# A decoder layer on one core: other DMA layouts for its weights and for queries and keys, and a redrawn order of work

## The chip, the cores and the metric

The kernel runs on one core of one Trainium2 chip. The metric is the device time in microseconds, lower is better. A core has TensorE (PE, with its weight loads as PEld), VectorE (DVE), ScalarE (ACT), GpSimd (POOL) and SyncE (SP), which here issues every DMA. SBUF is the on-chip memory, PSUM the accumulator memory of PE.

## The reference, cut to what matters

The input `x` is 16 sequences of 256 rows of 512 float32 numbers. The layer adds three things to it, one after the other:

```python
x = x + attn(layernorm(x), q_w, q_b, k_w, k_b, v_w, v_b, o_w, o_b)       # 16 heads of 32, causal
x = x + xattn(ctx_2048, ctx_2048, layernorm(x), ssm_kernel, D, 8)
x = x + ffn(layernorm(x), w_gate_up, w_down)

# attn: q = x @ q_w.T + q_b, likewise k, v; softmax(q k^T / sqrt(32) + causal mask) @ v, then @ o_w.T + o_b
# xattn: per head h (8 rows i, j): kv[i,j] = k[i] * v[j]; y = causal convolution of kv with ssm_kernel[h]
#        out[j] = sum_i (y[i,j] + D[h] * kv[i,j]) * q[i]
# ffn: activations and weights rounded to 8 bits per row; silu(gate) * up, then down
```

## The kernel before, in words

The work has two halves. In the first, 16 batches of attention are cut into 64 units `(b, g)`: a batch of 256 rows and a group of four heads. In the second, 32 tiles of 128 rows go through the convolution and the FFN. Beside the attention the pair products `kv` of the convolution are made (`pairs_*`) and the FFN weights are rounded and turned (`weight_*`).

At the start the four projection weights are loaded in float32 (`proj_in`, `wl_q` to `wl_o`, 1 MB each), squared and summed on ACT for a bound of their size (`proj_norm`), from which scales come (`scale_top`, `scale_all`: short DVE instructions and two tiny matmuls). Each weight is turned on PE against an identity (`proj_turn`, sixteen 128x128 blocks), and written to SBUF as the sum of two float16 parts: `proj_hi` on ACT and `proj_lo` on DVE. Every projection is then three matmuls, high times high, high times low, low times high (`mm3`).

For each batch the rows are loaded (`norm_load`, step `xi`), normalised (`norm_stats`, `norm_rows`), split into a high part on ACT (`turn_hi`, `xh`) and a low part on POOL (`turn_lo`, `xl`), and both are turned by a DMA (`turn_out`, steps `("xo", b, 0)` and `("xo", b, 1)`, into `xhT` and `xlT`). Finished rows are stored by `out_store` (`os`); the buffer `xt` of a batch is one of three.

For each unit, `project_mm` computes queries and keys, `project_hi` and `project_lo` split them in two float16 parts each (`qkhl`, four planes of 128x256), `project_store` writes them to DRAM (`qk_d`, step `qs`), and `project_stack` reads them back in five DMAs into `st` (`qt`), where the parts of 32 rows stand above each other so that one matmul of 96 rows gives the scores. Then come softmax, the turning of the probabilities and the weighted sum.

The order of the instructions on every engine is not written by hand. Each step is given to a planner (`Plan.add`) with its engine, a due time (`when`), a planned duration, the steps it comes after, and the buffers it takes. `Plan.order` walks planned time; whenever an engine is free it starts the ready step with the earliest due time. The program is emitted in that order, so each engine's queue, that of SP among them, is fixed by it. With `T = 8.8` planned microseconds a unit, batch `b` has `t = 4 * T * b`; steps of the changeover and the second half follow from `B2 = 64 * T`. A table `shift` then moves the due times: for every kind of step (the first part of its key and the length of the key) one value for each range of `when`, the ranges cut at `bounds`:

```python
for s in pl.steps:
    if isinstance(s["key"], tuple):
        v = shift.get((s["key"][0], len(s["key"])))
        s["when"] += v[sum(s["when"] >= b for b in bounds)] if v else 0.0
```

An argument `after=` makes a step wait for another's end with its DMA landed; `then=` only for the other's issue.

Of the kernel before, what the change touches and what calls it, by code (L numbers as in the profile page):

```python
# [11 lines left out]
F16 = mybir.dt.float16  # L12
I32 = mybir.dt.int32
AF = mybir.ActivationFunctionType
# [94 lines left out]
def kernel(  # L109
# [433 lines left out]
    if True:  # L543
# [50 lines left out]
        def proj_in(nm):  # L594
            wl = wld.tile([P, KC, D], F32, name=f"wl_{nm}")
            nc.sync.dma_start(wl, dict(q=q_w, k=k_w, v=v_w, o=o_w)[nm].rearrange("(o p) i -> p o i", p=P))
            wraw[nm] = wl
# [17 lines left out]
        def scale_top(j):  # L615
# [6 lines left out]
            nc.vector.tensor_scalar(t2[:, 2:4], idf[:2, :2], t2[:, 1:2], None, ALU.mult)  # L622
# [5 lines left out]
        def scale_all(j):  # L628
# [8 lines left out]
            nc.vector.tensor_tensor(bias[:, j:j + 2, :], bias[:, j:j + 2, :], ap(sc, j, [[1, 2], [0, KC]]), ALU.mult)  # L637
# [9 lines left out]

        def proj_hi(nm, kc):
            nc.scalar.activation(wT[nm][0][:, kc, :], wps[nm, kc], AF.Copy, scale=sc[:, 2, names.index(nm):names.index(nm) + 1])

        def proj_lo(nm, kc):
            hi, lo = wT[nm]
            nc.vector.scalar_tensor_tensor(
                lo[:, kc, :], wps.pop((nm, kc)), sc[:, 2, names.index(nm):names.index(nm) + 1], hi[:, kc, :],
                ALU.mult, ALU.subtract)
# [119 lines left out]
        def project_store(b, g):  # L775
            pjs.pop(("qk", b, g))
            qk_d = dram.tile([4, P, S], F16, tag="qk_d", bufs=4, name=f"qk_d{b}_{g}")
            nc.sync.dma_start(qk_d.rearrange("n p s -> p n s"), qks.pop((b, g)))
            qkd[b, g] = qk_d

        def project_stack(b, g, n):
            if n == 0:
                stks[b, g] = ap2.tile([96, 2, 4, S], F16, tag="st", bufs=STB, name=f"st{b}_{g}")
            r3, first, n, src = ((0, 0, 2, 1), (1, 0, 1, 1), (1, 1, 1, 3), (2, 0, 1, 0), (2, 1, 1, 2))[n]
            nc.sync.dma_start(
                stks[b, g][32 * r3:32 * r3 + 32].rearrange("r j h s -> r (j h) s")[:, 4 * first:4 * first + 4 * n, :],
                bass.AP(qkd[b, g].tensor, qkd[b, g].offset + src * P * S, [[S, 32], [32 * S, 4 * n], [1, S]]))


        def scores_mm(b, g, qc, h2):  # L790
# [8 lines left out]
            for hh in range(2):  # L799
                nc.tensor.matmul(  # L800
                    ps[:, hh, :nk], stk[:, 0, 2 * h2 + hh, qc * P:(qc + 1) * P], stk[:, 1, 2 * h2 + hh, :nk],
# [279 lines left out]
        for n, nm in enumerate(names):  # L1081
            j = n // 2
            pl.add(("pi", nm), "SP", -80 + 10 * n, 0.55, proj_in, nm, late=1.5, dma=3.3)
# [73 lines left out]
        def batch(b):  # L1157
            t = KC * T * b
            xt = ("xt", b)
            if True:  # L1160
                pl.add(("xi", b), "SP", t - 9.5 * T, 0.44, norm_load, b, late=1.9, dma=1.5, new=[xt])
                if b == 0:
                    pl.add("ob", "SP", -45, 0.5, bias_rows, late=2.0, dma=0.8)
# [117 lines left out]
        for i in range(NT):  # L1281
# [76 lines left out]
        bounds = (60,330,570,680,1010)  # L1358
        shift = {
            ("bi", 2): (0.8, 5.7, 3, 5.9, 1.9, 8.6),  # L1360
            ("bk", 3): (14.4, 12.2, -4.6, 11.1, 15.6, 13.5),
            ("bn", 2): (-4.8, 0.7, 13.6, -2.3, -10.8, 2.5),
            ("bp", 2): (0.2, -9, 3.2, 0, 2.1, 3.1),
            ("bq", 2): (8.5, -3.6, 0.7, 0.7, -24, 0.7),
            ("br", 2): (6.5, 6.7, 1.5, 1.5, -20.1, 1.5),
            ("bs", 2): (0.5, 0.5, 12, 0.5, 20.5, 11.6),
            ("bt", 2): (-3.1, 4.5, 6, 10.4, -3.2, -23.3),
            ("ck", 2): (-1.3, -3.1, -0.1, 0.4, -3.2, -0.3),
            ("cl", 3): (-2.5, 1.1, -0.3, 2.3, -4.4, 1.3),
            ("cm", 2): (-3.9, -1.5, -4.7, -1, -1.5, -4.8),  # L1370
            ("cm", 3): (-3.3, -0.5, 5.2, 4.4, 7.2, -7.4),
            ("co", 2): (-2.8, 5.1, -9.1, 6.1, -12.9, -12.1),
            ("cr", 2): (-4.6, 3.8, -1.4, 0.3, 0.6, 8),
            ("cs", 3): (-7.5, -6, -24.7, -8.3, -15.4, -9.2),
            ("ct", 3): (2, 2.5, 0.3, 0.3, 5.3, -0.5),
            ("cu", 3): (0.2, 1.3, -10.5, -7.1, -6.1, 10.5),
            ("cw", 2): (-1.4, 14, 15.9, -13.5, -1.4, -10.2),
            ("cx", 2): (-27.7, -25.8, -20.3, 0.1, -26.2, -22.6),
            ("cz", 2): (-0.6, 1.6, 0.1, -1.1, 0.1, 0.1),
            ("dm", 2): (9.4, 21.8, 4.5, 11.7, 42.3, 23.4),  # L1380
            ("do", 2): (6.5, -0.8, -1, -6.8, -0.7, -20.7),
            ("dr", 2): (17.3, 17, 7.9, 9, 24.4, 14.2),
            ("ds", 2): (-1.2, -1.7, 7, -1.7, -3.6, 4.7),
            ("fc", 3): (-1.3, 2.5, -6.8, -2.3, 1.7, 1.8),
            ("fd", 2): (-0.3, 0.4, -7.3, 2.9, 0.4, -2.9),
            ("fm", 2): (-14, -14, -17.7, -12.3, -15.4, -10.3),
            ("fm", 3): (1.6, 0.8, -2.2, -0.7, 6.5, 3.9),
            ("fn", 2): (0.2, 0.9, -0.7, 0.2, 2, -4.5),
            ("fo", 2): (2.3, -7.2, 16.2, 3.2, 1.4, -7.2),
            ("fp", 2): (6.6, -2.6, 6.6, -1.9, -11, -3.8),  # L1390
            ("fq", 2): (0.8, -4.2, 0.7, -3, 5.5, 0.8),
            ("fr", 2): (-4.7, 2.6, -0.2, 8.5, 5.7, -28.6),
            ("fs", 2): (-0.1, -20.6, -16.5, 0.2, -23.3, -16.9),
# [106 lines left out]
```

## Time and profile before

| | |
|---|---|
| time, median of 3 runs | 1157.89 us (1155.21 to 1161.72) |
| profiled execution | 1164.23 us, of which the span is 1162.4 us |
| PE busy | 1076.4 us (93%) |
| DVE busy | 1015.8 us (87%) |
| POOL busy | 947.5 us (82%) |
| ACT busy | 838.0 us (72%) |
| DMA | 229.48 MB in 269026 packets |

The profile is one execution. Its span is the time between the first and the last instruction, and the execution's own time lies 1.8 us above it. Busy is the share of the span in which an engine has at least one instruction under way. Matmuls overlap: one of 256 columns is recorded at about 0.27 us, while the next starts 0.11 us later, so a busy PE is not yet PE at its peak. The first matmul of the convolution starts at 621.6 us.

### The profile page before, as it was taken

The numbers are of one execution on the slowest core, as the hardware profiler recorded it, in microseconds if no ns is written. First come the engines' busy times: TensorE is split into PE (matmuls) and PEld (weight loads), VectorE is DVE, ScalarE is ACT, GpSimd is POOL, SyncE is SP. The second block draws the span as 40 slices with busy tenths as digits, with TensorE's granted clock in tenths as the row PEclk, the third lists the DMA queues.
The fourth block names the chain that finished last, engine by engine and source line by source line (L and its number), as shares of the span: only waits on it lengthen the run. The fifth ranks groups of instructions, "written<-read, shape, count | busy, mean of one in ns | idle before, by whom it ended". The sixth has DMA issues, their size and how long they took to land.

```text
span 1162.4 us, 25593 instructions
## 1 busy us (share of the span) xinstructions
PE 1076.4 (93%) x8503; PEld 766.8 (66%) x8503; DVE 1015.8 (87%) x3188; ACT 838.0 (72%) x1999; POOL 947.5 (82%) x924
## 2 busy tenths in 40 slices
PE   4999889999999989999999889999999999999965
PEld 3766657776667756776666666767767667766632
DVE  5999678888788877987787999999999999999997
ACT  6898878898998878998885456575556566655444
POOL 4497888889999966899514799999999999999962
PEclk9999999999999999999999999999999999999989
DMA  7687798888888977879548956657666766676422
GB/s 244 166 226 246 207 225 219 246 262 229 229 245 233 264 215 199 251 228 258 172 145 274 280 153 189 186 148 192 168 175 169 186 167 168 174 187 156 102 48 66
DMA packets 269026, 229.48 MB, mean 197 GB/s; under 512 B 125177, under 2 KB 223519, under 8 KB 268767
## 3 DMA queue, kind: packets, MB, share of 16 engines
q1 hardware_dynamic: 268895, 227.85, 70.4%
q8 instruction: 67, 1.10, 0.4%
q14 instruction: 64, 0.52, 0.1%
HBM read 124.10 MB, written 75.74 MB: 172 GB/s over the span
## 4 chain that ended last, share of the span: by engine, by line
DVE 32%; PE 31%; POOL 13%; ACT 9%; DMA 8%; issue 5%; SPq 2%; DVEq 0%; POOLq 0%; ACTq 0%
DVE hp L450 4%; PE g L425 4%; ACT p L816 3%; DVE s L454 3%; DVE u L338 3%; DVE p L809 3%; PE pj_qk L659 3%; PE pj_qk L658 3%; PE pj_qk L660 3%; DMA xlT<-xl 2%; DVE u L341 2%; PE c L324 2%; PE c L326 2%; PE c L325 2%; POOL g L443 2%
## 5 line engine op out<-in xcount | busy, mean ns | idle before, releaser
L816 ACT ACTIVATE p<-p,nmax 128x256 f32<-128x256 f32 (+1 forms) x512 | 230.0, 454 | 11.3 <-DVE nmax L809 10.7
L809 DVE CUSTOM_DVE_ANT_0 p<-s,mask,esc 128x128 f32<-128x128 f32 (+1 forms) x512 | 187.1, 411 | 14.8 <-PE s L800 14.6
L324 PE MATMUL c<-bkv,T 128*128 128x288 f16 x640 | 183.2, 286 | 9.4 <-issue 3.2
L325 PE MATMUL c<-bkv,T 128*128 128x288 f16 x640 | 183.1, 286 | 0.0
L326 PE MATMUL c<-bkv,T 128*128 128x288 f16 x640 | 183.0, 286 | 0.0
L425 PE MATMUL g<-w,xq 128*128 128x384 bf16 (+1 forms) x1024 | 169.1, 315 | 13.1 <-DVE o L528 6.3
L964 POOL TENSOR_TENSOR kv<-p,kv 128x1152 f16<-128x1152 f32 x64 | 152.0, 2382 | 7.9 <-ACT kv L959 7.8
L946 POOL TENSOR_TENSOR p<-kT 128x1024 f32<-128x1024 f32 x64 | 143.9, 2249 | 2.3
L425 PEld LDWEIGHTS <-xq 128*128 128x128 bf16 x1024 | 100.4, 98 | 68.0 <-issue 8.1
L443 POOL TENSOR_TENSOR g<-g,sw 128x704 f32<-128x704 f32 x60 | 101.0, 1705 | 3.9 <-ACT g L436 3.9
L816 ACT ACTIVATION_READ_ACCUMULATOR p<-p,nmax 128x1 f32 x512 | 100.4, 196 | 0.0
L800 PE MATMUL s<-st 96*128 96x128 f16 (+1 forms) x512 | 84.5, 247 | 8.9 <-DVE nmax L809 8.4
L338 DVE TENSOR_TENSOR u<-c,qT 128x512 f32<-128x512 f32 x128 | 87.3, 682 | 5.9 <-PE c L326 5.3
L766 ACT ACTIVATE qkhl<-pj_qk,bias 128x256 f16<-128x256 f32 x128 | 59.8, 469 | 45.3 <-PE pj_qk L660 33.7
L771 DVE SCALAR_TENSOR_TENSOR qkhl<-pj_qk,bias,qkhl 128x256 f16<-128x256 f32 x128 | 59.9, 478 | 33.5 <-ACT qkhl L766 21.0
L827 POOL TENSOR_SCALAR lb<-lsum 128x256 f32<-128x256 f32 x64 | 26.0, 406 | 75.6 <-DVE lsum L823 48.9
L357 POOL TENSOR_TENSOR u<-u 128x512 f32<-128x512 f32 x60 | 76.9, 1282 | 9.6 <-DVE u L338 9.6
L510 PE MATMUL d<-w,hq 128*128 128x512 bf16 x352 | 80.9, 379 | 3.8 <-DVE hp L450 3.0
L324 PEld LDWEIGHTS <-T 128*128 128x128 f16 x640 | 62.6, 98 | 29.1 <-DVE u L344 5.9
L659 PE MATMUL pj_qk<-xlT,wq_hi 128*128 128x256 f16 x256 | 70.5, 275 | 10.7 <-DMA xlT<-xl 10.7
L841 PE MATMUL pt<-idf,p 128*128 128x128 f32 x524 | 79.9, 275 | 0.0
L658 PE MATMUL pj_qk<-xhT,wk_hi 128*128 128x256 f16 x256 | 70.0, 273 | 7.3 <-ACT qkhl L766 6.9
(236 smaller groups left out, 3326.1 us busy)
## 6 DMA issues: line engine op xcount, KB each, us to landing
kv_d<-kv SPq DMA_DIRECT2D x64, 576.0 KB, 3.5
bkv<-kv_d SPq DMA_DIRECT2D x64, 576.0 KB, 3.9
qk_d<-qkhl SPq DMA_DIRECT2D x64, 256.0 KB, 2.9
st<-qk_d SPq DMA_DIRECT2D x256, 64.0 KB, 2.7
T<-pad_d SPq DMA_DIRECT2D x64, 256.0 KB, 4.2
x_d<-xt SPq DMA_DIRECT2D x32, 256.5 KB, 3.5
bx<-x_d SPq DMA_DIRECT2D x32, 256.5 KB, 3.6
xt<-in_x_dram SPq DMA_DIRECT2D x16, 512.0 KB, 4.2
```

Of the source, the lines that this page charges most:

```text
L324: nc.tensor.matmul(reg, T[:, 0, d:d + P], kv[:, mi, 0, :], start=mi == 0, stop=False)
L325: nc.tensor.matmul(reg, T[:, 0, d:d + P], kv[:, mi, 1, :], start=False, stop=False)
L326: nc.tensor.matmul(reg, T[:, 1, d:d + P], kv[:, mi, 0, :], start=False, stop=mi == li)
L338: nc.vector.tensor_tensor(ap(u, uo, [[UW, 2], [64, 4], [1, 64]]), ap(pc, 0, [[512, 2], [64, 4], [1, 64]]), ap(qT, qo, [[96, 2], [8, 4], [1 ...
L425: nc.tensor.matmul(pg[:, :c.stop - c.start].rearrange("p (r o) -> p r o", o=P), t["xq"][:, kc, :], w1[:, (o + c.start) // P:(o + c.stop) / ...
L443: (nc.gpsimd if i < NT - 2 else nc.vector).tensor_tensor(ts[i]["g1"][:, c], ts[i]["g1"][:, c], sw1[:, I + c.start:I + c.stop], ALU.mult)
L658: nc.tensor.matmul(ps, lh, rh, start=first, stop=False)
L659: nc.tensor.matmul(ps, lh, rl, start=False, stop=False)
L809: nc.vector.tensor_tensor_reduce(out=prs[b, g][qc][:, h, :], in0=ps[:, hh, :nk], in1=mask2[:, P - qc * P:2 * P], op0=ALU.add, op1=ALU.min, ...
L816: nc.scalar.activation(pr[:, h, :], pr[:, h, :], AF.Exp, scale=-1.0, bias=nmax[:, qc, h:h + 1], accum_out=lsum[:, qc, h:h + 1])
L946: nc.gpsimd.tensor_tensor(ap(p, 0, [[NKV, 4], [64, 4], [1, 64]]), ap(kT, o, [[96, 4], [0, 4], [1, 64]]), ap(kT, o, [[96, 4], [8, 4], [1, 6 ...
L964: nc.gpsimd.tensor_tensor(kv[:, :, 1, :], p, kv[:, :, 0, :], ALU.subtract)
```

## The change

Seven edits:

1. `proj_in` puts row `4p + o` of a weight into partition `p`, where before it was row `128o + p`. A partition's four rows are then one piece of 8 KB in DRAM, where they were four of 2 KB. The turned blocks hold every fourth column, and `proj_hi` and `proj_lo` write (and read `hi`) with a step of four float16 elements, so that `wT` is as before.
2. The load of the output weights is issued after the first batch's `xlT` transpose: `then=[("xo", 0, 1)]` for the fourth weight.
3. `qk_d` is laid out `[128, 4, 256]` in place of `[4, 128, 256]`: a partition's four planes are one piece of 2 KB.
4. `st` is laid out `[96, 4, 2, 256]`, heads before query and key, so that the stack read which takes two planes has pieces of 1 KB; the four others keep pieces of 512 B, now 2 KB apart in DRAM.
5. Two multiplications by a scale use `scalar_tensor_tensor` with a broadcast operand in place of `tensor_scalar` and `tensor_tensor`.
6. The planner is told 2.9 instead of 3.3 us of DMA for a projection weight, and 2.0 instead of 0.5 us of SP for `ob`.
7. `bounds` has two cuts more, at -50 and 10, and all values of `shift` are others.

```diff
-            nc.sync.dma_start(wl, dict(q=q_w, k=k_w, v=v_w, o=o_w)[nm].rearrange("(o p) i -> p o i", p=P))
+            nc.sync.dma_start(wl, dict(q=q_w, k=k_w, v=v_w, o=o_w)[nm].rearrange("(p o) i -> p o i", p=P))
...
-            nc.vector.tensor_scalar(t2[:, 2:4], idf[:2, :2], t2[:, 1:2], None, ALU.mult)
+            nc.vector.scalar_tensor_tensor(t2[:, 2:4], idf[:2, :2], 1.0, ap(t2, 1, [[0, 2]]), ALU.mult, ALU.mult)
...
-            nc.vector.tensor_tensor(bias[:, j:j + 2, :], bias[:, j:j + 2, :], ap(sc, j, [[1, 2], [0, KC]]), ALU.mult)
+            nc.vector.scalar_tensor_tensor(bias[:, j:j + 2, :], bias[:, j:j + 2, :], 1.0, ap(sc, j, [[1, 2], [0, KC]]), ALU.mult, ALU.mult)
...
+        def cols(t):
+            return t.rearrange("k (p o) -> k o p", o=KC)
+
         def proj_hi(nm, kc):
-            nc.scalar.activation(wT[nm][0][:, kc, :], wps[nm, kc], AF.Copy, scale=sc[:, 2, names.index(nm):names.index(nm) + 1])
+            nc.scalar.activation(cols(wT[nm][0][:, kc, :]), wps[nm, kc].rearrange("k (o p) -> k o p", o=KC), AF.Copy,
+                                 scale=sc[:, 2, names.index(nm):names.index(nm) + 1])
...
-                lo[:, kc, :], wps.pop((nm, kc)), sc[:, 2, names.index(nm):names.index(nm) + 1], hi[:, kc, :],
-                ALU.mult, ALU.subtract)
+                cols(lo[:, kc, :]), wps.pop((nm, kc)).rearrange("k (o p) -> k o p", o=KC),
+                sc[:, 2, names.index(nm):names.index(nm) + 1], cols(hi[:, kc, :]), ALU.mult, ALU.subtract)
...
-            qk_d = dram.tile([4, P, S], F16, tag="qk_d", bufs=4, name=f"qk_d{b}_{g}")
-            nc.sync.dma_start(qk_d.rearrange("n p s -> p n s"), qks.pop((b, g)))
+            qk_d = dram.tile([P, 4, S], F16, tag="qk_d", bufs=4, name=f"qk_d{b}_{g}")
+            nc.sync.dma_start(qk_d, qks.pop((b, g)))
...
-                stks[b, g] = ap2.tile([96, 2, 4, S], F16, tag="st", bufs=STB, name=f"st{b}_{g}")
-            r3, first, n, src = ((0, 0, 2, 1), (1, 0, 1, 1), (1, 1, 1, 3), (2, 0, 1, 0), (2, 1, 1, 2))[n]
+                stks[b, g] = ap2.tile([96, 4, 2, S], F16, tag="st", bufs=STB, name=f"st{b}_{g}")
+            r3, j, w, src = ((0, 0, 2, 1), (1, 0, 1, 1), (1, 1, 1, 3), (2, 0, 1, 0), (2, 1, 1, 2))[n]
...
-                stks[b, g][32 * r3:32 * r3 + 32].rearrange("r j h s -> r (j h) s")[:, 4 * first:4 * first + 4 * n, :],
-                bass.AP(qkd[b, g].tensor, qkd[b, g].offset + src * P * S, [[S, 32], [32 * S, 4 * n], [1, S]]))
+                stks[b, g][32 * r3:32 * r3 + 32].rearrange("r h j s -> r h (j s)")[:, :, j * S:(j + w) * S],
+                bass.AP(qkd[b, g].tensor, qkd[b, g].offset + src * S, [[4 * S, 32], [32 * 4 * S, 4], [1, w * S]]))
...
-                    ps[:, hh, :nk], stk[:, 0, 2 * h2 + hh, qc * P:(qc + 1) * P], stk[:, 1, 2 * h2 + hh, :nk],
+                    ps[:, hh, :nk], stk[:, 2 * h2 + hh, 0, qc * P:(qc + 1) * P], stk[:, 2 * h2 + hh, 1, :nk],
...
-            pl.add(("pi", nm), "SP", -80 + 10 * n, 0.55, proj_in, nm, late=1.5, dma=3.3)
+            pl.add(("pi", nm), "SP", -80 + 10 * n, 0.55, proj_in, nm, late=1.5, dma=2.9, then=[("xo", 0, 1)] * (n == 3))
...
-                    pl.add("ob", "SP", -45, 0.5, bias_rows, late=2.0, dma=0.8)
+                    pl.add("ob", "SP", -45, 2.0, bias_rows, late=2.0, dma=0.8)
...
-        bounds = (60,330,570,680,1010)
+        bounds = (-50,10,60,330,570,680,1010)
         shift = {
...
-            ("os", 3): (-2.5, 6.4, 18.1, 4, 7.2, 14.8),
+            ("os", 3): (-7.4, -2.2, -6.8, 2.1, 1.1, -0.6, 2.1, 3.7),
...
-            ("pl", 2): (4, 12.2, -5.9, 12.2, 1.3, -1.8),
+            ("pl", 2): (18.4, -8.3, 19, 28.7, 5.1, 25.2, 19.8, 16.8),
...
-            ("qm", 3): (0, 1.9, -1.6, -1.4, -1.6, -1.4),
+            ("qm", 3): (2.8, 1.8, -0.3, 2.1, -1, 4.3, -12.4, -0.7),
...
-            ("xh", 2): (1, -0.1, -0.1, -0.1, 32.8, 1),
-            ("xi", 2): (-29.5, 8.3, 8.2, -18.2, 5.6, -45.6),
-            ("xl", 2): (-1.3, -1.4, -1.6, 3, 0.8, 2.4),
-            ("xo", 3): (-36.7, -30.1, 24.9, -48.9, -48.1, -40.2),
+            ("xh", 2): (3.4, 3.9, -4.4, 17.4, -1.5, 6.2, 6, 6),
+            ("xi", 2): (-24.3, -17.4, -2, -1.1, -23.8, -10.5, -0.3, -23.8),
+            ("xl", 2): (-1.9, -7.1, 0, -15, -4.1, -9.5, -9.8, -15),
+            ("xo", 3): (-20.3, -21.3, 37.5, -20.3, 38.2, -18.1, -30.3, -18.2),
...
```

The table has 98 kinds of steps; the lines shown are those that the prediction speaks of. In the old table the ranges are below 60, 60 to 330, 330 to 570, 570 to 680, 680 to 1010 and above; in the new one, below -50, -50 to 10, 10 to 60, and then the same.

## The prediction

> **What bounds the kernel now.** I read the page first, then the busy time by stretches, then who waits for whom on PE and on the SP queue, then the start in order of time and the chain that ended last, then the DMA rates of two quiet stretches. From the page:
>
> ```profile
> span 1162.4 us, 25593 instructions
> PE 1076.4 (93%) x8503; PEld 766.8 (66%) x8503; DVE 1015.8 (87%) x3188; ACT 838.0 (72%) x1999; POOL 947.5 (82%) x924
> PE   4999889999999989999999889999999999999965
> DMA  7687798888888977879548956657666766676422
> DVE 32%; PE 31%; POOL 13%; ACT 9%; DMA 8%; issue 5%; SPq 2%; DVEq 0%; POOLq 0%; ACTq 0%
> ```
>
> PE is busy for 1076 us of 1162, and the chain is split between DVE and PE: a kernel that runs against its matmuls, with VectorE close behind. What can be won lies where PE is idle. The busy time by stretches (the second number is the length, the third PE) says where:
>
> ```profile
> 0.00:15.00 15.00, 3.07 (x13) 2.60 (x13) 5.64 (x23) 7.64 (x8) 4.66 (x13) 1.00 0.82 297
> 100.00:200.00 100.00, 91.01 (x773) 64.97 (x772) 79.47 (x311) 83.02 (x248) 80.14 (x65) 0.98 0.83 221
> 400.00:500.00 100.00, 92.42 (x798) 66.11 (x796) 83.38 (x325) 84.71 (x259) 76.47 (x62) 0.98 0.79 225
> 700.00:800.00 100.00, 99.09 (x715) 70.50 (x713) 97.26 (x246) 61.56 (x87) 93.51 (x105) 1.00 0.65 172
> 1125.00:1163.00 38.00, 23.72 (x139) 12.68 (x137) 29.21 (x65) 19.10 (x25) 8.24 (x7) 0.95 0.26 56
> ```
>
> Length minus PE, summed over such stretches: 17.7 us in 0 to 60, 42.7 us in 60 to 700 (attention and the changeover), 4.3 us in 700 to 1100, 21.9 us in the tail. The 400 us of convolution and FFN hold nothing for an order of work to win; the tail is DVE at 52.3 of 63 us, whose instructions are the same in both kernels. So the change is decided in the start and in attention. There PE waits mostly for one thing, and SP for another (us in total, times, longest):
>
> ```profile
> PE pj_qk L659 <- DMA xlT<-xl: 10.7, 6, 3.7
> PE s L800 <- DVE nmax L809: 8.4, 18, 1.7
> PE pj_qk L658 <- ACT qkhl L766: 6.9, 9, 1.1
> SPq L785 <- DMA qk_d<-qkhl: 72.4, 41, 4.8
> ```
>
> The chain shows the same (start, duration): the low halves of the turned rows arrive just when the projections need them.
>
> ```profile
> 123.40 5.90 DMA xlT<-xl
> 154.76 6.93 DMA xlT<-xl
> 423.06 6.15 DMA xlT<-xl
> ```
>
> **The change part by part.**
>
> *Output weights behind the first turned rows.* The start in order of time:
>
> ```profile
> 4.37 1.97 SPq L596 DMA_DIRECT2D wl_o<-in_L_attn_o_w_dram  x1
> 6.38 2.62 SPq L592 DMA_DIRECT2D ob<-in_L_attn_o_b_dram  x1
> 12.97 3.18 SPq L718 DMA_TRANSPOSE xhT<-xh  x1
> 16.25 3.54 SPq L718 DMA_TRANSPOSE xlT<-xl  x1
> 21.93 0.75 DVE L653 SCALAR_TENSOR_TENSOR wq_lo<-wq,sc,wq_hi 128x512 f16<-128x512 f32 x1 [0.67 <-ACT wq_hi L649]
> 25.36 0.42 PE L658 MATMUL pj_qk<-xhT,wq_hi 128*128 128x256 f16 x1
> ```
>
> The two first transposes take 3.18 and 3.54 us to issue, where the next pair takes 1.24 and 1.23: they stand behind 1 MB of wl_o, which nobody reads before 25.33 (its square on ACT). Without wl_o ahead, ob issues about 2 us earlier, and xlT's issue, which can begin when xl is made (15.14), ends near 16.4 instead of 19.8. It is moved past ob, the third xt load and both transposes on SP; its one issue (0.5 to 2 us) then falls before the next pair at 21.27, with 1.5 us of SP idle there. At 1 MB in about 2.6 us it lands near 21, with 4 us to spare; were it later, ACT would stand at that square with the first projections' high halves behind it. Of the 3.4 us only a part counts: the first projection could not start before wq_lo ends (22.68), and starts at 25.36, because twelve turnings of wk and wv are ahead of it. Ceiling 2.7 us. The new first columns of the shift table (ranges before -50 and before 10) redraw just this part; I take 2 us, between 0 and 3.
>
> *Weights in 8 KB rows.* The rates of the stretch 3 to 12 us, nearly all 2 KB pieces:
>
> ```profile
> DMA packets 1538, 2.98 MB, mean 331 GB/s; under 512 B 74, under 2 KB 86, under 8 KB 1538
> q1 hardware_dynamic: 1538, 2.98, 89.7%
> ```
>
> That is 0.897 x 16 x 9 us / 1538 = 84 ns a packet, and the best slices of that stretch run at 400 to 428 GB/s. The Trainium skill, "DMA: Bandwidth & Descriptors", section "Where 436 GB/s comes from", puts the HBM side at about 358 GB/s, by which nothing is left and the loads would be slower than they are; the slices are above it, so the measurement decides, and the other limit of that section, 435, leaves some 6%: 0.15 us per MB. wl_q is the first link of the chain (6.1 us), so 0.2 us; at no cost to the later ones, which wait in ACT's order. The price of the new row order is the strided write of hi and lo: 16 ACT instructions of 0.67 us (L649) and 16 DVE of 0.75 (L653), now with 8 bytes between elements. No row here writes so. Nearest row: the same two, unchanged. From below: no faster[...]; from above: twice, 22.7 us, of which about half would be on the start's path. The skill's "SBUF — State Buffer", section "Specifications (TRN2)", lets accesses run at full rate with two hits per 16-byte line, and 8-byte steps are two hits; no run here shows it yet. I take 0, and keep +11 as an end.
>
> *Queries and keys in 2 KB pieces.* 64 stores go from 512 to 128 packets, and one of five stack reads from 256 to 128 packets. The stretch 582 to 592 us holds almost nothing else:
>
> ```profile
> GB/s 107 0 0 0 0 0 264 285 285 213 68 0 0 0 0 29 125 252 264 148 172 98 195 62 195 35 0 0 0 0 0 0 115 378 386 173 0 0 0 0
> DMA packets 1550, 0.96 MB, mean 96 GB/s; under 512 B 128, under 2 KB 1408, under 8 KB 1549
> ```
>
> The store issued at 582.59 moves in five quarter-microseconds at 285 GB/s at best, about 1.0 us. The same skill page (section "Specifications") gives 512 B as the smallest piece at line rate: by the rule the store gains nothing. By the trace 2 KB pieces run at 400 GB/s and 512 B pieces at 285: 262 KB take 0.65 instead of about 0.95 us, -0.3 us of some 2.3. I take the trace. What hides it: most stores are read by a later unit. On the chain a store with its stack stands three times, so -0.9 us; from below 0 (all hidden), from above -6 us, if a third of the 64 stores should count with their 0.3 us. The reads now take 512 B at a 2 KB pitch; their issue (0.43 us each) paces them, not the bytes: 0.
>
> *Scale products.* Four small DVE instructions change form (0.22 us at L622, 0.17 at L637; nearest other form 0.15 to 0.28 at L608): within ±0.2 us on the start's path. `ob`'s planned 2.0 us and the weights' 2.9 only move planned times.
>
> *The order.* Every step's due time is redrawn, so every queue is. What bears on the 10.7 us: in the range 60 to 330 x-low's subtraction (`xl`, on POOL) is due at t-63.4-15.0 instead of t-63.4-1.4, and the pair products' subtraction (`pl`, POOL, 2.4 us) 16.5 us later. In the trace, xl of the batch at 147 us ran at 150.1 although its input was there at 148.2, behind a pair product. In 330 to 570 the store of finished rows (`os`) is due 17 us earlier and the next load of rows into the freed buffer (`xi`) 32 us earlier; both stand on the chain at 209 and 278 us. These loosen the loop that makes xlT late. Against it: `xh` is due 17.5 us later in 60 to 330, and `xo` 9.8 and 13.3 us later in the two ranges. I take two thirds of the wait, -7 us, and nothing for the rest of the 42.7 us, since the trace can't rank it.
>
> Sum: -2.0 -0.2 -0.9 -7 = -10.1 us against the profiled execution's own 1164.23 us (span 1162.4 and 1.8 around it), -0.87%. That execution is 0.55% above the median of the runs, so on 1157.89 it is 1148.
>
> **The rivals.** *The turned rows come later instead.* For the batches whose `xo` falls in 330 to 570 (11 to 15), it is now due at t-52.8+38.2 = t-14.6, while the first projection that reads it is due at t-32.7; before it was t-27.9. SP then takes every store, stack and load that is due in those 13 us first. The price: up to the largest wait seen, 3.7 us, on each of five batches, 18 us, with the 3 us of the other edits won: +15 us, 1172. For it: SP already keeps PE waiting in this stretch (423 us). Against it: a due time only ranks what is ready, and SP has idle time. It decides when PE's wait for xlT passes about 20 us instead of 10.7; under 14 it can't carry a loss.
>
> *A shuffle.* The waits of 60 to 700 are many and small (43 us in some hundred), and a new order trades them one for one. Then only the start and the stores remain: -3 us, 1155, no change that shows. For it: after 700 us nothing moves at all, 99% of PE.
>
> *A large win.* Half of the 42.7 us goes, the start gives 3, the tail 5: -29 us, 1129. Against it: DVE is at 80 to 86% and POOL above 90% in parts of that stretch, so it is not PE's queue alone.
>
> **How the numbers follow.** About 0.5% (5.8 us) is what a measurement of this kernel can tell from no change. The likely case 0.43, the large win 0.07, the shuffle 0.17, later turned rows (and redrawn orders that lose elsewhere) 0.33. Faster 0.50, same 0.17, slower 0.33. As both signs hold much, the likely case's own range is 1138 to 1153. The range for 8 in 10 is 1130 to 1177: down to the large win's edge, up to the slower rival's 1172 with the strided writes part-way to their bound.
>
> **What would show it.** Right: the first projection at 22.5 to 24 us; the first xhT and xlT issue in 1.3 us each; PE's wait for xlT at 4 us or less; packets near 235,000; SP's wait for qk_d under 60 us; L649 and L653 at 0.65 to 0.8 us. Wrong: xlT's wait above 14 us, L649 or L653 above 1 us, PE idle in 60 to 700 above 45 us, or more than 2 us of change in 700 to 1100.

## The result, and the profile after

The changed kernel takes 1174.28 us (median of 4 runs, 1172.33 to 1177.91); the kernel before takes 1157.22 us on the same chip (1155.21 to 1161.72). The ratio is 1.0140, 95% interval 1.0109 to 1.0171: 17 us slower (16 by the ratio), where 10 us faster was forecast. The profiled execution of after took 1173.82 us (span 1172.0). That of before was one of the longer of its runs (1164.23), so the two profiles differ by 9.6 us only. For a fairer pair I also use the profile of before with the new stores alone (an experiment below): its span is 1157.4 us, and its start is that of before within 0.3 us.

The page of after: span, PE's busy time, PE by fortieths, packets, the chain that ended last.

```profile
span 1172.0 us, 25577 instructions
PE 1077.8 (92%) x8503; PEld 765.0 (65%) x8503; DVE 1023.8 (87%) x3188; ACT 846.5 (72%) x1999; POOL 947.9 (81%) x924
PE   3888999999999989999999889999999999999965
DMA packets 234722, 229.48 MB, mean 196 GB/s; under 512 B 125177, under 2 KB 182559, under 8 KB 233951
DVE 30%; PE 26%; POOL 17%; DMA 10%; ACT 8%; issue 5%; SPq 2%; DVEq 0%; POOLq 0%; ACTq 0%
```

PE does the same work in a longer span. DVE and ACT are each 8 us busier with the same number of instructions, so some instructions have become longer. The clock granted to PE is not the cause: its mean is 0.994, and was 0.993 before. The shares of the chain tell nothing here: with the order of before, POOL has 13% of it in one kernel and 29% in another (before, and the new stores alone). PE's row says more: its first four digits are each one lower than before's, and its second half is digit for digit the same.

Busy time by stretches of after (second number the length, third PE, then PEld, DVE, ACT, POOL):

```profile
15.00:30.00 15.00, 6.50 (x27) 4.62 (x27) 13.58 (x27) 12.76 (x13) 7.54 (x4) 1.00 0.71 162
60.00:100.00 40.00, 33.32 (x309) 25.14 (x307) 35.74 (x127) 31.71 (x94) 35.00 (x29) 1.00 0.76 193
100.00:200.00 100.00, 94.77 (x823) 67.28 (x821) 84.88 (x337) 87.40 (x261) 83.77 (x70) 1.00 0.76 230
700.00:800.00 100.00, 99.05 (x715) 70.51 (x715) 97.28 (x249) 62.91 (x88) 93.03 (x107) 1.00 0.64 175
```

The same view of before, for the two stretches that the prediction did not show:

```profile
15.00:30.00 15.00, 10.87 (x66) 9.37 (x67) 10.05 (x31) 11.79 (x16) 7.64 (x5) 1.00 0.66 177
60.00:100.00 40.00, 37.34 (x335) 26.75 (x333) 38.84 (x136) 36.53 (x115) 37.68 (x31) 1.00 0.82 236
```

PE loses 4.4 us in 15 to 30 and 4.0 us in 60 to 100, gains some back in 100 to 200, and is untouched after 700. The first unit's weighted sum is copied out of PSUM (`lt`, a mark of when that unit is done) at 66.9 us instead of 56.8; the first matmul of the convolution starts at 630.9 instead of 621.6. From there both kernels take 541 us to the end. So the loss lies in the start and in attention.

The waits of after (us in total, times, longest):

```profile
PE pj_qk L664 <- DMA xlT<-xl: 4.7, 6, 1.6
PE s L806 <- DVE nmax L815: 7.7, 16, 1.1
SPq L791 <- DMA qk_d<-qkhl: 51.0, 32, 5.3
```

The two waits that the change was forecast to shorten did shorten: PE's for xlT from 10.7 to 4.7 us, SP's for the stored queries and keys from 72.4 to 51.0. The time went elsewhere. The wait for xlT varies between kernels: seven others that keep the order of before in attention (experiments below) show 6.6 to 9.5 us.

And the start of after, in order of time:

```profile
12.57 1.35 SPq L723 DMA_TRANSPOSE xhT<-xh  x1
14.77 2.01 SPq L723 DMA_TRANSPOSE xlT<-xl  x1
15.53 2.34 POOL L706 TENSOR_TENSOR xt<-xt,ob 128x1024 f32<-128x1024 f32 x1 [0.79 <-DMA ob<-in_L_attn_o_b_dram]
15.89 1.99 DVE L622 SCALAR_TENSOR_TENSOR t<-idf,t 2x2 f32<-2x2 f32 x1
16.83 0.58 SPq L596 DMA_DIRECT2D wl_o<-in_L_attn_o_w_dram  x1
19.00 1.41 ACT L653 ACTIVATE wq_hi<-wq,sc 128x512 f16<-128x512 f32 x1 [0.81 <-DVE sc L634]
19.50 1.15 DVE L637 SCALAR_TENSOR_TENSOR bias<-bias,sc 128x8 f32<-128x8 f32 x1
21.69 1.34 DVE L658 SCALAR_TENSOR_TENSOR wq_lo<-wq,sc,wq_hi 128x512 f16<-128x512 f32 x1
28.45 0.42 PE L663 MATMUL pj_qk<-xhT,wq_hi 128*128 128x256 f16 x1
```

The transposes issue earlier and quicker, as forecast, and yet the first projection starts 3.1 us later. Two things are new on its way. The high and low halves of the weights take 1.41 and 1.34 us, where they took 0.67 and 0.75. And a product of four numbers (L622) takes 1.99 us instead of 0.22, and ends at 17.88, when POOL's addition of the output bias (L706) ends at 17.87.

### The profile page after: what moved, and what is told of

The parts are those of the page before. It is cut to its first block, busy times and chain, and to the rows that moved or that the text cites. A ratio compares the mean times of both kernels' runs of the same rounds, so it can differ in the third digit from the quotient of the medians.

```text
span 1172.0 us, 25577 instructions
## 1 busy us (share of the span) xinstructions
PE 1077.8 (92%) x8503; PEld 765.0 (65%) x8503; DVE 1023.8 (87%) x3188; ACT 846.5 (72%) x1999; POOL 947.9 (81%) x924
## 2 busy tenths in 40 slices
DMA packets 234722, 229.48 MB, mean 196 GB/s; under 512 B 125177, under 2 KB 182559, under 8 KB 233951
## 4 chain that ended last, share of the span: by engine, by line
DVE 30%; PE 26%; POOL 17%; DMA 10%; ACT 8%; issue 5%; SPq 2%; DVEq 0%; POOLq 0%; ACTq 0%
PE g L425 4%; DVE hp L450 3%; DVE s L454 3%; DVE u L338 3%; DVE p L815 2%; ACT p L822 2%; PE c L324 2%; POOL g L443 2%; PE c L326 2%; PE c L325 2%; POOL p L952 2%; PE pj_qk L663 2%; PE pj_qk L664 2%; DVE u L341 2%; POOL kv L970 2%
## 5 line engine op out<-in xcount | busy, mean ns | idle before, releaser
L815 DVE CUSTOM_DVE_ANT_0 p<-s,mask,esc 128x256 f32<-128x256 f32 (+1 forms) x512 | 187.8, 410 | 11.6 <-PE s L806 10.9
L806 PE MATMUL s<-st 96*128 96x256 f16 (+1 forms) x512 | 84.6, 247 | 12.9 <-DVE nmax L815 7.7
L965 ACT CAST kv<-p 128x1152 f16<-128x1152 f32 x64 | 73.5, 1148 | 12.3 <-DMA kv_d<-kv 6.9
L847 PE MATMUL pt<-idf,p 128*128 128x128 f32 x512 | 77.2, 273 | 2.5 <-ACT t L855 1.5
L806 PEld LDWEIGHTS <-st 96*128 96x128 f16 x512 | 46.4, 98 | 43.8 <-issue 23.4
```

The costliest lines, as they stand in the source:

```text
L806: nc.tensor.matmul(ps[:, hh, :nk], stk[:, 2 * h2 + hh, 0, qc * P:(qc + 1) * P], stk[:, 2 * h2 + hh, 1, :nk], start=True, stop=True)
L815: nc.vector.tensor_tensor_reduce(out=prs[b, g][qc][:, h, :], in0=ps[:, hh, :nk], in1=mask2[:, P - qc * P:2 * P], op0=ALU.add, op1=ALU.min, ...
```

## The experiments

Each ratio below is against before in runs on the same chip, with its 95% interval. Before itself took 1157 to 1162 us there, so expectations given in us are read by the ratio. Line numbers are those of each kernel.

### The order and the layouts, each alone

`new_order_old_layouts` is after with the 2 KB weight rows, the old halves, stores and scale products put back: only the order of steps is new. `old_order_new_layouts` is the reverse: the order of before with all the new layouts and products. In the other three one part is undone or done alone:

```diff
 # after_rows_undone: after with the weight rows and the halves of before
-dma_start(wl, ....rearrange("(p o) i -> p o i", p=P))
+dma_start(wl, ....rearrange("(o p) i -> p o i", p=P))
 # after_scale_undone: after with the scale products of before
-nc.vector.scalar_tensor_tensor(t2[:, 2:4], idf[:2, :2], 1.0, ap(t2, 1, [[0, 2]]), ALU.mult, ALU.mult)
+nc.vector.tensor_scalar(t2[:, 2:4], idf[:2, :2], t2[:, 1:2], None, ALU.mult)
 # before_store: before with the 2 KB stores and their reads alone
-qk_d = dram.tile([4, P, S], F16, ...)
+qk_d = dram.tile([P, 4, S], F16, ...)
```

> The changed kernel's order (its table, its planner numbers, output weights behind the first turned rows) with the old layouts and old forms of the four loads, of queries and keys, and of the scale products: edits 1, 3, 4 and 5 undone, the queues in the same order as in the changed kernel. If the start's slower instructions (strided writes of the weight halves, scale products that take 1 to 2 us) are the cause, the 10 us by which the first unit is late go away: 1160 to 1166 us, first lt copy near 57 us. If the redrawn order is the cause, it stays at 1172 to 1176.

> The kernel before with edits 1, 3, 4 and 5 (8 KB rows with strided writes, the 2 KB pieces, the scale products' form), its queues in the old order. If the layouts are the cause: L649 and L653 of the old numbering at 1.4 and 1.35 us instead of 0.67 and 0.75, the first unit 6 to 10 us late, 1163 to 1172 us. If the order is the cause: 1154 to 1159 us.

> The changed kernel with edit 1 alone undone (2 KB rows again, weight halves written without a step), same order. If the strided writes carry the loss: 16 x 0.74 us less on ACT and 16 x 0.6 us less on DVE, of which those of q and k (8 x 0.74 = 6 us) lie on the start's path: 1166 to 1169 us. If the scale products or the order carry it: 1172 to 1176.

> The changed kernel with edit 5 alone undone (tensor_scalar and tensor_tensor again), same order. If the new form is what makes L622 wait until POOL's norm_bias ends (1.99 us, ending together with it): L622 back at 0.22 us, the scales 1.8 us earlier, 1171 to 1173 us. If the old form waits for POOL just as well in this order: L622 stays near 2 us and the time at 1174.

> The kernel before with edits 3 and 4 alone (queries and keys stored in 2 KB pieces), its queues in the old order. If a store that moves about 0.3 us sooner counts where the chain goes through it: 1155 to 1159 against 1159 to 1160 of the kernel before, 34,304 minus 1,536 packets fewer, SP's wait for qk_d from 72 to about 55 us. If it is hidden: no difference.

| kernel | ratio to before | first unit's copy, us |
|---|---|---|
| new_order_old_layouts | 1.0083 (1.0061 to 1.0105) | 57.0 |
| old_order_new_layouts | 1.0063 (1.0044 to 1.0081) | 63.4 |
| after_rows_undone | 1.0064 (1.0039 to 1.0088) | 59.9 |
| after_scale_undone | 1.0128 (1.0109 to 1.0146) | 66.8 |
| before_store | 0.9988 (0.9974 to 1.0002) | 56.8 |
| after | 1.0140 (1.0109 to 1.0171) | 66.9 |

So there are two causes, of about the same size, and they add up (0.83% and 0.63%, against 1.40% for both together). The new order alone loses 9.6 us, with a start that is no later than before's; at 1169.64 us it fell between the two ranges expected. The new layouts alone lose 7 us, all of it visible at the first unit, and PE loses nothing more behind it (600.5 us busy in 60 to 700, where `before_store` has 601.7). Within the layouts it is the weight rows: undone, after falls by 0.76%. The stores are worth -1.4 us (the interval just reaches no change), where -0.9 was forecast. What they do not do is shorten SP's wait for the stored queries and keys:

```profile
SPq L786 <- DMA qk_d<-qkhl: 70.0, 42, 4.5
SPq L786 <- DMA qk_d<-qkhl: 57.3, 37, 5.2
```

The first row is of `before_store`, where about 55 us was expected; the second, of `new_order_old_layouts`, has the old stores. So most of the fall from 72.4 to 51.0 came with the order. The form of the scale products is worth nothing that shows: in `after_scale_undone` the old form, too, took 2.02 and 1.11 us in place of 0.22 and 0.17, and in `old_order_new_layouts` the new form took 0.15 and 0.17.

### Which part of the weight rows costs

The rows bring two things: 8 KB pieces for the DMA, and columns out of order, which the halves put back by writing float16 with 8 bytes between elements. Three kernels keep the 8 KB rows and restore the order of columns elsewhere.

```diff
 # rows_read_strided (on before), after_rows_read (on after): the halves read PSUM with a step, write contiguously
+nc.scalar.activation(wT[nm][0][:, kc, :].rearrange("k (p o) -> k p o", o=KC),
+                     wps[nm, kc].rearrange("k (o p) -> k p o", o=KC), AF.Copy, scale=...)   # the low half likewise
 # rows_pe_strided (on before): PE's transposes write PSUM with a step of 16 bytes, the halves are before's
-nc.tensor.transpose(wps[nm, kc][:, oc * P:(oc + 1) * P], ...)
+nc.tensor.transpose(wps[nm, kc].rearrange("k (p o) -> k o p", o=KC)[:, oc, :], ...)
```

> Kernel before (old order) with the 8 KB weight rows alone; the halves put the columns back in order by reading PSUM with a step (o innermost) and writing their fp16 rows contiguously. Theory W (it is the fp16 write at an 8-byte step that doubles the halves): w_hi stays near 0.67 us and w_lo near 0.75, the first unit's lt copy at 56 to 58 us, time 1155 to 1159. Rival S (any step on either side costs the double): w_hi 1.4, w_lo 1.35, lt copy at 62 to 64 us, 1164 to 1167. Rival R (not the halves but the 8 KB rows themselves, late to land): halves 0.67 and 0.75 and still 1164 to 1167.

> Kernel before (old order) with the 8 KB weight rows alone; TensorE's transposes write their 128 columns into PSUM at a step of 16 bytes, ACT and DVE read and write as in before. Theory W: halves 0.67 and 0.75, time 1155 to 1159, unless the transposes take longer for the step: they took 4 x about 0.11 us a group in before; double would be 16 x 0.44 = +7 us of PE, of which the start's idle PE hides most: at most +3. Rival R: 1164 to 1167.

> Changed kernel with the 8 KB weight rows, but the halves read PSUM with the step and write fp16 contiguously. Theory (after = the order's 9 us + the strided writes' 7 us - the stores' 1.4): the writes' part goes, halves 0.67 and 0.75, first unit's lt copy at 57 to 60 instead of 66.9 us, time 7 us under after: 1165 to 1169 on a chip where before has 1158, ratio 1.006 to 1.009. Rival (after's start is late by its order, not by the halves): 1172 to 1176, ratio 1.012 or more.

Measured: `rows_read_strided` 1.0002 (0.9986 to 1.0018), `rows_pe_strided` 0.9991 (0.9971 to 1.0011), `after_rows_read` 1.0061 (1.0038 to 1.0083). Groups by shape (instructions, then total and mean ns), first of `old_order_new_layouts`, which writes with the step:

```profile
L652 ACT ACTIVATE wq_hi<-wq,sc 128x512 f16<-128x512 f32 x3 | 4.2, 1402 | 0.0
L657 DVE SCALAR_TENSOR_TENSOR wq_lo<-wq,sc,wq_hi 128x512 f16<-128x512 f32 x3 | 4.1, 1371 | 2.3 <-ACT wq_hi L652 2.3
```

then of `rows_read_strided`, which reads with it:

```profile
L649 ACT ACTIVATE wq_hi<-wq,sc 128x512 f16<-128x512 f32 x3 | 2.0, 675 | 0.0
L655 DVE SCALAR_TENSOR_TENSOR wq_lo<-wq,sc,wq_hi 128x512 f16<-128x512 f32 x3 | 2.2, 749 | 1.5 <-ACT wq_hi L649 1.5
```

Same rows, same elements, same order of work. Written at an 8-byte step the halves take 1402 and 1371 ns. Read from PSUM with the step (four float32 numbers 512 bytes apart, then the next four) and written in one piece they take 675 and 749 ns, against 675 and 748 in before. PE's writes at a 16-byte step cost nothing that shows either: the first three groups of four transposes of wl_q start 0.91 and 0.85 us apart, in before 0.91 and 0.86. So the rows are innocent and the stepped float16 access to SBUF is the cause. On ACT that is the write alone. On DVE it is the write together with the read of `hi`, which has the same step; no run parts these two.

The recorded durations overlap when such instructions follow each other: in after ACT starts one every 1.14 us (0.57 in before), DVE every 1.14 to 1.16 (0.66). So the 16 x 0.73 us of ACT and 16 x 0.6 us of DVE, 21 us of recorded time, are some 8 to 9 us of busy time on each engine. At the end the step is worth 1.0140 - 1.0061 = 0.79% in after, 9 us, with 0.4% of uncertainty on a difference of two ratios; 8 us of it stand at the first unit (copied at 58.8 instead of 66.9 us).

### The output weights' fetch, alone

To move steps without a new plan, the order of before was written out as a list and edited. `wl_o_moved` puts the fetch of wl_o behind the first turned rows and moves nothing else; `wl_o_ob_moved` does the same with the bias rows `ob`, ahead of wl_o.

```diff
-for s in pl.order():
-    s["fn"](*s["args"])
+for k in ORDER:            # the order of before
+    s = pl.by[k]
+    s["fn"](*s["args"])
 # wl_o_moved:    ... ("xo", 0, 1), ("pi", "o"), ...
 # wl_o_ob_moved: ... ("xo", 0, 1), "ob", ("pi", "o"), ...
```

> Kernel before with its old layouts and its own order, written out; only the step that fetches wl_o stands behind the first turned rows (after the xlT transpose), no other step moves. Theory O (the changed order costs by what else it moved, not by this fetch): first xhT transposes issue at about 1.4 and 2 us, xlT wait on PE 10.7 to about 5 us, time 1154 to 1158. Rival F (the later fetch itself costs, as ob lands earlier and norm_bias on POOL then locks the scale products for 2 us, or wl_o's halves come late): scale product at 2.0 us instead of 0.22, first unit's lt copy later than 57 us, 1160 to 1166.

> As wl_o_moved, with the bias rows' fetch ob moved behind the first turned rows too, ahead of wl_o. Theory P (DVE's small product waits for POOL's norm_bias that runs at the time, and norm_bias starts when ob lands): norm_bias starts at 18.5 us or later, the product is back to about 0.22 us, first qk matmul 1.5 to 2.4 us ahead of wl_o_moved's 25.97, time 1155 to 1159 where before has 1158, since a gain of 1 us at the start was not seen in the time of rows_read_strided. Rival (the product is slow for its form or its operands): again 2 us and more, and the first qk matmul at 26.

Measured: 1.0000 (0.9981 to 1.0019) and 0.9999 (0.9981 to 1.0016), so a change of 2 us either way would not show. In `wl_o_moved` the two transposes issue in 1.36 and 2.23 us, as theory O has it, but PE's wait for xlT is 8.3 us and not 5; the product takes 2.42 us, as rival F has it, but the time is not longer. The start of `wl_o_moved` in order of time:

```profile
15.96 2.42 DVE L1100 TENSOR_SCALAR t<-idf,t 2x2 f32<-2x2 f32 x1
16.02 2.35 POOL L1179 TENSOR_TENSOR xt<-xt,ob 128x1024 f32<-128x1024 f32 x1 [1.20 <-DMA ob<-in_L_attn_o_b_dram]
17.13 0.57 SPq L1074 DMA_DIRECT2D wl_o<-in_L_attn_o_w_dram  x1
```

and of `wl_o_ob_moved`:

```profile
16.54 0.22 DVE L1100 TENSOR_SCALAR t<-idf,t 2x2 f32<-2x2 f32 x1
17.75 0.42 SPq L1074 DMA_DIRECT2D wl_o<-in_L_attn_o_w_dram  x1
21.89 2.35 POOL L1179 TENSOR_TENSOR xt<-xt,ob 128x1024 f32<-128x1024 f32 x1 [6.60 <-DMA ob<-in_L_attn_o_b_dram]
```

With wl_o out of its way `ob` lands early, POOL starts its addition beside DVE's product, and the product lasts as long as the addition (both end at 18.37 to 18.38 us). With `ob` late, POOL starts at 21.89 and the same instruction takes 0.22 us. The Trainium skill, "SBUF — State Buffer", section "Who interferes with whom", has a rule that fits the new form: a DVE instruction with two inputs in SBUF contends with a GpSimd instruction that reads SBUF, and the section calls this an exclusive lock. The rows agree. The old form, which multiplies one input by a factor per partition, is held as well (2.42 us); why, no run here shows. Short instructions with constants (L633 to L635, 0.14 to 0.15 us at 18.75 to 19.31 in after) ran beside POOL unhindered.

The expectation of `wl_o_ob_moved` missed in one number. Its first projection started at 25.28 us, 0.7 ahead of `wl_o_moved`, and not 1.5 to 2.4. Measured from the arrival of wl_q (ACT's first square, at 8.60 and 8.13 us), it is 16.7 against 17.8 us, and 16.9 in before and 16.6 in `before_store`. So even without the lock the earlier transposes bring nothing that shows: the way to the first projection goes through the scales, the halves and PE's turnings of the weights, not through xlT. The lock itself, 1.1 us at the first projection, is gone by the end (1.0000 against 0.9999).

### Where the order loses

The new order with old layouts, with part of its table of due times put back (each column of the eight is a range of planned time, each row a kind of step), or with a part of one order spliced to a part of the other (the first 277, 1085 or 2256 steps, up to 60, 184 or 366 us of planned time):

```diff
 # cols_60_330_old, cols_330_570_old: one column of the table of new_order_old_layouts from before
 # xo_old: one row of it from before
-("xo", 3): (-20.3, -21.3, 37.5, -20.3, 38.2, -18.1, -30.3, -18.2),
+("xo", 3): (-36.7, -36.7, -36.7, -30.1, 24.9, -48.9, -48.1, -40.2),
 # new_60_then_old and the like: ORDER = first part of one order, then the rest of the other
```

> new_order_old_layouts (1169.6 us), but the table's values for due times from 330 to 570 are the old ones. By the progress of PE, that kernel loses 7 us against the old order between 280 and 560 us, bit by bit. If the new values of this range are the cause: 1162 to 1165 us. If the loss comes from what the range before leaves behind, or any redrawing costs it: 1168 to 1171.

> new_order_old_layouts, but the table's values for due times from 60 to 330 are the old ones. That kernel falls back by 8 us between 65 and 140 us of the trace and wins 5 of it back before 190. If the range's values cost nothing on balance: 1167 to 1171 us. If the range carries the loss: 1160 to 1164.

> new_order_old_layouts with the old values of one kind of step alone, the DMA transposes xo, in all ranges. If the prediction's rival holds (turned rows due after other work of SP in 330 to 570), 4 to 8 us come back: 1162 to 1166, with PE's wait for xlT going down. PE's wait for xlT in the changed kernel is only 4.7 us against 10.7 before, which speaks against it: then 1167 to 1171.

> Kernel before with its old layouts; the steps are emitted from a written-out list: the changed order for its first 277 steps (planned time 60 us), then the remaining ones in the order of before. Theory A (the start itself costs: wl_o moved behind, norm_bias beside the scale products): all of the order's +8 to +10 us is here, 1165 to 1168. Theory B (the loss lies later, where POOL falls behind between 280 and 560 us): the start is worth -2 to 0 us as new_order_old_layouts was 1.7 us ahead at 65 us: 1155 to 1159.

> As new_60_then_old, with the changed order for the first 1085 steps (planned time 184 us). Theory B: +2 us as the whole changed order stood at 189 us, 1158 to 1161. Theory C (the 5 to 8 us lost between 85 and 137 us are what is never got back): 1163 to 1168. Theory A: 1165 to 1168 as in new_60_then_old.

> As new_60_then_old, with the changed order for the first 2256 steps (planned time 366 us). Theory B with a loss that grows evenly over 280 to 560 us: about half, 1161 to 1164; if one place between 370 and 430 us does it (ACT qkhl behind PE pj_qk 4.7 us): within 2 us of before. Theory A and C: 1165 to 1168.

> Kernel before with its old layouts; the order of before for the steps up to planned time 184 us, then the remaining ones in the changed order. Theory B: most of the order's loss, 1164 to 1168. Theories A and C: none of it, 1156 to 1159.

| kernel | ratio to before |
|---|---|
| new order whole (new_order_old_layouts) | 1.0083 (1.0061 to 1.0105) |
| xo_old | 1.0086 (1.0060 to 1.0112) |
| cols_330_570_old | 1.0156 (1.0123 to 1.0189) |
| cols_60_330_old | 1.0204 (1.0173 to 1.0235) |
| new_60_then_old | 1.0077 (1.0055 to 1.0098) |
| new_184_then_old | 1.0043 (1.0023 to 1.0062) |
| new_366_then_old | 1.0138 (1.0105 to 1.0171) |
| old_184_then_new | 1.0063 (1.0039 to 1.0087) |

`xo_old` speaks against one rival: with the turned rows due as in before the time stays the same, and PE waits 4.9 us for xlT. The two column experiments, both slower than the ranges expected, say little about the columns, since the planner redraws everything behind a changed due time. The splices do not redraw, but a seam can cost too: up to 366 us of new order cost 16 us, more than the whole. So a splice alone does not say where the whole order loses, and its stretches have to be looked at. PE's busy time in 60 to 200 and in 200 to 600 us, of `before_store`, `new_60_then_old` and `new_order_old_layouts`:

```profile
60.00:200.00 140.00, 128.89 (x1108) 91.53 (x1106) 118.04 (x446) 120.33 (x365) 118.58 (x97) 0.99 0.80 228
200.00:600.00 400.00, 381.90 (x3348) 276.56 (x3347) 330.62 (x1284) 354.95 (x1076) 331.44 (x267) 1.00 0.77 227
60.00:200.00 140.00, 123.83 (x1078) 88.04 (x1077) 118.09 (x442) 117.00 (x352) 118.86 (x95) 0.99 0.78 221
200.00:600.00 400.00, 382.01 (x3319) 276.06 (x3318) 328.32 (x1279) 354.24 (x1075) 333.29 (x268) 1.00 0.80 229
60.00:200.00 140.00, 128.25 (x1090) 89.99 (x1088) 117.86 (x452) 118.34 (x358) 116.53 (x93) 0.98 0.78 219
200.00:600.00 400.00, 374.22 (x3276) 270.19 (x3275) 322.83 (x1248) 348.31 (x1050) 333.82 (x268) 1.00 0.81 228
```

The splice loses 5 us before 200 and nothing behind it. The whole new order loses 0.6 us before 200 and 7.7 behind it (5.4 against the profile of before, which has 379.6 us there). After shows the same against `old_order_new_layouts`: 0.4 us, then 5.5. So the whole order's loss lies between 200 and 600 us, and what the first 60 us of it cost in the splice, it makes good itself. Theory B comes nearest: `old_184_then_new`, 7.3 us slower, is in its range. It failed for `new_60_then_old`, since the tail of before does not make the start good. Theories A and C, by which the start holds the whole loss, do not fit these rows.

What the new start costs shows in 60 to 100 us, first `before_store`, then `new_60_then_old`:

```profile
60.00:100.00 40.00, 37.53 (x337) 26.93 (x335) 38.60 (x136) 36.30 (x114) 37.68 (x31) 1.00 0.77 232
60.00:100.00 40.00, 33.60 (x288) 23.77 (x287) 36.90 (x125) 33.50 (x101) 36.15 (x31) 0.96 0.68 208
```

All eight kernels with the new first 60 us (after among them) have 33.3 to 35.9 us of PE there, and the nine with the old ones 36.5 to 37.6, even `old_order_new_layouts`, whose first unit is copied at 63.4 us, later than the splice's (58.6). Nor is it PE's clock, 0.96 in the second row: after has 1.00 there and the same loss. What happens, in order of time, in `before_store`:

```profile
59.89 1.05 POOL L1050 TENSOR_SCALAR qb<-qw 128x1024 bf16<-128x1024 f32 x1
62.35 1.24 SPq L1056 DMA_TRANSPOSE qt<-qb  x1
63.98 0.94 SPq L968 DMA_DIRECT2D kv_d<-kv  x1
64.19 0.88 DVE L771 SCALAR_TENSOR_TENSOR qkhl<-pj_qk,bias,qkhl 128x256 f16<-128x256 f32 x2 [0.27 <-ACT qkhl L766]
65.46 1.19 SPq L778 DMA_DIRECT2D qk_d<-qkhl  x2
```

and in `new_60_then_old`:

```profile
65.17 1.65 DVE L1249 SCALAR_TENSOR_TENSOR qkhl<-pj_qk,bias,qkhl 128x256 f16<-128x256 f32 x4
66.72 1.06 POOL L1527 TENSOR_SCALAR qb<-qw 128x1024 bf16<-128x1024 f32 x1
67.80 1.25 SPq L1533 DMA_TRANSPOSE qt<-qb  x1
70.14 0.35 SPq L1445 DMA_DIRECT2D kv_d<-kv  x1
71.03 1.02 SPq L1256 DMA_DIRECT2D qk_d<-qkhl  x2
```

POOL ends the rounding `qb` of FFN weights 6.8 us later. SP's queue has a fixed order: its transpose of `qb`, which attention does not need, waits for POOL, the store of pair products behind it waits for POOL again, and only then comes the store of queries and keys that the next units' scores need, 5.6 us later than in `before_store`. Of these, 1.7 us are DVE's, which ends the low halves at 66.8 instead of 65.1; from there the store stands 4.2 us at SP, where it stood 0.4. This is read from the trace; that no other wait of this stretch would have cost the same was not tried.

Which wait costs the 5 to 8 us behind 200 stays open. It is not known to be one: the work of the pair products is put off to the end of attention (the last `kv_d` stores at 584 us in `new_order_old_layouts`, 567 in `before_store`), but no run brings it forward alone.

### A version of what did not cost

`best` is the order of before with `ob` and wl_o behind the first turned rows, 8 KB rows with contiguous halves, the 2 KB stores, and the old scale products.

```diff
+ the halves and rows of rows_read_strided
+ qk_d = dram.tile([P, 4, S], F16, ...)   # and its reads, as in before_store
+ ORDER of wl_o_ob_moved
```

> Order of before with ob and wl_o behind the first turned rows, 8 KB weight rows with halves written contiguously, and the stores in 2 KB pieces; scale products in their old form. Each part alone was worth 0 to -1.4 us: first qk matmul at 22 to 24 us, first lt copy at 53 to 55, sum -1 to -4 us: 1154 to 1157 where before has 1158, ratio 0.9965 to 0.9995. If the start's gain is eaten by the queues behind it as in rows_read_strided, only the stores' -1.4 stays.

Measured: 1158.67 us (1152.43 to 1161.01) where before had 1161.90, ratio 0.9963 (0.9942 to 0.9984). It beats the kernel before by 0.4%. The parts, each alone, sum to 0.1%, so where the rest comes from stays open. The first projection starts at 24.57 us and the first unit's copy at 55.8, later than the 22 to 24 and 53 to 55 expected.

## Why the prediction was wrong

Two terms of the sum failed, and either of them takes the forecast gain away.

**Strided writes: taken at 0, measured +9 us; this step failed.** The prediction set the nearest row, the same halves unchanged, against a bound of twice, 22.7 us, with half of it on the start's path. It chose 0, leaning on the Trainium skill, "SBUF — State Buffer", section "Specifications (TRN2)": two hits to a 16-byte line run at full rate. The measurement decides against that: 0.67 to 1.41 us on ACT and 0.75 to 1.34 on DVE, nearly the upper bound in recorded time, and 7 to 9 us at the end. "About half on the start's path" was right too (10 us at the first unit in after, of which the halves are 8). The nearest row was not near: it had the operation but not the access pattern, which was what was new. L649 or L653 above 1 us was named as a sign of being wrong, and it came.

**The order: taken at -7, measured +9.6; this is the larger miss.** The prediction read 10.7 us of waiting for xlT as time to be won, and put nothing for the rest of the 42.7 us of idle PE. Both halves failed. PE's busy time in 60 to 700 us, of before and of `new_order_old_layouts`:

```profile
60.00:700.00 640.00, 597.34 (x5123) 430.86 (x5121) 535.60 (x1955) 525.30 (x1546) 513.37 (x439) 0.99 0.80 228
60.00:700.00 640.00, 591.39 (x5068) 423.56 (x5066) 528.94 (x1942) 522.35 (x1541) 509.63 (x433) 0.99 0.79 227
```

The wait for xlT fell from 10.7 to 6.5 us. The rest of PE's idle time rose from 32.0 to 42.1. The fall was won where it did not count: in 60 to 200 us, where before waits 5.4 us for xlT and the new order not at all, PE was busy as long in both; in 200 to 600, where the time was lost, the wait is 6.5 us against 5.3. Other waits took its place. Which ones, behind 200 us, the runs leave open.

**The output weights: taken at -2, measured 0, with 2 us either way.** wl_o issued as worked out (at 16.83, in 0.58 us) and so did the first transpose (1.35); the second took 2.01 us where 1.3 was forecast. That no gain came is read from the start: the ceiling of 2.7 us was no ceiling of this edit, as the turnings of the weights that hold the first projection stay where they are. And the earlier `ob`, which the prediction named without a cost, let POOL's addition fall on the scale product.

**Scale products: within ±0.2.** Their form is worth nothing, as said. Their 1.8 and 1.0 us more in after come with POOL's two additions, which end at 17.87 and 20.62 us as the products do (17.88 and 20.65), and with neither form.

**Stores: taken at -0.9, measured -1.4** (-3.0 to +0.2), and packets at 234,722, as forecast. The reading behind it set loads of 2 KB pieces against stores of 512 B; a store of 2 KB pieces in `before_store`, issued at 578.57 us, does reach 391 GB/s where 285 was seen. SP's wait for qk_d fell below 60 us, but by the order. Nothing moved behind 700 us, as forecast.

**The 8 KB rows themselves: -0.2 forecast**, too little for these runs to show (1.0002, 0.9986 to 1.0018). ACT's first square, which waits for wl_q, starts at 7.7 and 7.9 us in `rows_read_strided` and `rows_pe_strided` (8.1 in `best`), against 8.1 to 8.7 in five kernels with 2 KB rows and the start of before.

**The rivals.** "The turned rows come later" gave 1172, close to the measured 1174, by luck: PE's wait for xlT fell, and `xo_old` changed nothing. "A shuffle" had waits traded one for one; in the new order alone they grew by some 6 us. The range for 8 in 10 (1130 to 1177) held, in part for the reason given, the strided writes.

## What to carry to other kernels

When a layout change saves packets, ask first who now writes with a step. Let the step fall on a PSUM read or on PE's PSUM write, which were free here, and keep float16 accesses to SBUF contiguous. A transfer that lands earlier starts its consumer earlier, and on POOL that can hold a tiny DVE instruction for as long as POOL's instruction lasts (here without a cost at the end). And a redrawn order has to be measured by itself, apart from the layout that it comes with: the longest wait that it removes says little about its sum. A splice of two orders shows what a part costs in front of the other's rest; what it costs in its own order is read from the whole order's trace.

## What the runs showed of the hardware

- A float16 write to SBUF with 8 bytes between elements halves the rate of ACT (128x512 in 1.41 instead of 0.67 us, one every 1.14 instead of 0.57). On DVE the same write, with a float16 read at the same step, takes 1.34 instead of 0.75 us. A float32 PSUM read with 512 bytes between elements (675 and 749 ns) and transposes that write PSUM at 16 bytes (a group of four every 0.85 to 0.91 us) cost nothing that shows.
- A DVE instruction on 2x2 elements took up to 2.42 us beside a POOL addition of 128x1024, and 0.15 to 0.22 without it.
